# A four-layer graph network on one core: constant tiles for row numbers and list places, queries in two parts, layer 0's keys in another PSUM bank and its u8 conversions behind the copies

## The chip, the cores and the metric

The kernel runs on one core of a Trainium2 chip. The metric is the device time of one execution in microseconds (us); lower is better. The engines are named as in the profile: PE is TensorE (matmuls; PEld its weight loads), DVE is VectorE, ACT is ScalarE, POOL is GpSimd, SP is SyncE, which here only issues DMAs. Each engine takes its instructions from a queue of its own, and engines wait for one another by semaphores.

## What is computed

A node matrix x of 4096 x 256 and a symmetric 0/1 adjacency of 4096 x 4096 (about 0.8% ones) go through four graph layers, each followed by a residual add and a layer norm. All of it is fp32.

```python
# layer 0
deg = adj.sum(1, keepdims=True)
x = LN(x + relu(concat([x, adj @ x / max(deg, 1)]) @ W0 + b0))
# layer 1: two steps; R = (adj + I) / row sums, A = top-p attention
for n in range(2):
    q, k = Xa @ W1.T @ W2.T, Xa @ W3.T
    probs = softmax(q @ k.T)
    A = probs on the smallest set of largest entries whose mass reaches 0.9, renormalised
    Xf, Xa = R @ Xf, A @ Xa
    Z += Xf @ U1[n].T + Xa @ U2[n].T
x = LN(x + LN(x + Z))
# layer 2
x = LN(x + concat([x, adj @ x, diag(adj @ adj)]) @ W2 + b2)
# layer 3
x = LN(x + relu(D^-1/2 (adj + I) D^-1/2 @ x @ W3 + b3))
```

## The kernel before

Rows are worked in NT = 32 tiles of 128. A matrix that multiplies the adjacency is kept as an upper and a lower half in fp32r side by side, so one product with a 128 x 128 block of the adjacency is a matmul of 512 columns into one PSUM bank.

The code is traced tile by tile and a scheduler then fixes the order of each engine's queue: mainly the order of the text, with later instructions put forward where earlier ones are expected to wait. Buffers come from pools: a name (tag) with `bufs` buffers is used in turn, and an instruction that writes a buffer waits until the readers of its former content are done.

**Layer 0** (lines 207 to 297). `l0_main(it)` loads the tile's adjacency from POOL's queue in four pieces of 512 KB (L129; four buffers in all, so exactly one tile), and TensorE runs 32 matmuls over them (L160). `partial` does three things with each piece: ACT casts it to u8 (L234, two buffers) and SP stores that to DRAM for layer 1 (L235); DVE adds it into `sums` (L239, L241, L244). A piece's buffer is free when matmuls, cast and sums are done with it. `l0_degrees` makes the degree with a one-column matmul (L251), then its clipped reciprocal (`rd`), `rs` = 1/(deg + 1) and `dinv` = (deg + 1)^-0.5, the last on POOL (L259). `l0_agg` scales the product; `l0_end` loads x again (L270, on ACT's queue), transposes x and the product on TensorE (L170), copies the result from PSUM on ACT (`xt`, L172), multiplies with W0 (L274), and does bias, relu, residual and norm on DVE with the power on POOL (L184), and stores x1 and x1b by SP (L282, L283). `l0_keys` transposes the new rows, copies (L172), multiplies with W3 (L201), and splits the keys into an upper and a lower half (`upk` L194, L203 on ACT, L204 on DVE). L201 and L274 both write `mm_bank`, one PSUM bank used in two halves by turns. In iteration `it` of the loop the order of the text is: degrees and product of tile it-1, main of tile it, keys of tile it-2, end of tile it-1.

**Layer 1** (lines 300 to 994). `run_step` goes through the tiles with a pipeline of three: in iteration i, tile i+2 gets its logits (`logits_chunk`, L358: two matmuls for each of eight chunks g of 512 keys, then a copy to `e` on ACT, L359); tile i+1 is judged (row maximum from MAX8 of each group L377, exponentials L396/L400, the largest entries L472/L474, threshold, `flag`); tile i is multiplied (gathered rows in step 0, L616 and L703; transposed probabilities in step 1, L686 and L711). R times Xf runs beside it (L629, L632) and in step 0 the diagonal for layer 2 (L638, with the adjacency loaded again, L129). A dictionary `ops` hangs small pieces of work behind chunk g: `at(g, f)`. Among these: g = 1 is `mix` for the tile finished before (L764), g = 4 is `flag`, and g = 6 is `query` of tile i+3: transpose, copy (L172), matmul with the joined W1, W2 into `mm_bank` (L338), upper half on DVE (`upk`, L194), cast on ACT (L341) and lower half on DVE (L342). The q that comes out is what L358 of the next iteration multiplies.

`flag` (L526) decides which rows of a tile need another treatment and writes their row numbers into a list in DRAM (`list_d`) by an indirect DMA from POOL (L550): `at` holds each row's place in the list (L543) and `ids` its row number (L544), both tiles of 128 x 1 made anew for each tile, with four buffers. `ids` is computed from the constant `spare` and the tile's number alone. Rows on the list are worked through by `put_off` and `left_over` later.

**Layers 2 and 3** (lines 997 to 1061) run the adjacency product again, tile by tile; the change leaves them alone, but for `dinv` that they read.

Of the kernel before, what the change touches and what calls it, by code (L numbers as in the profile page):

```python
# [2 lines left out]

# [1 line left out]

# [6 lines left out]
F32 = mybir.dt.float32  # L12
I32 = mybir.dt.int32
# [8 lines left out]
P = 128  # L22
# [26 lines left out]
def gnn_stack(ctx, tc, x, adjt, adjn, w0, b0, w1, w2t, w3t, u1t, u2t, ln_g, ln_b, w2, b2, w3, b3, out):  # L49
# [114 lines left out]
    def transposed(*srcs):  # L164

        n = 2 * len(srcs)
        ps = ps_tr.tile([P, 4, P], F32, tag="tr", name="tr")
        for s, src in enumerate(srcs):
            for c in range(2):
                nc.tensor.transpose(ps[:, 2 * s + c, :], src[:, c * P : (c + 1) * P], ident)  # L170
        t = work.tile([P, 4, P], F32, tag="xt", name="xt")
        nc.scalar.copy(t[:, :n, :], ps[:, :n, :])  # L172
        return t

    def ln_stats(t):
# [20 lines left out]

    def make_keys(xt, dst):

        ps = half("mm")
        for c in range(2):  # L200
            nc.tensor.matmul(ps[:, :P], w3t_sb[:, c, :], xt[:, c, :], start=(c == 0), stop=(c == 1))  # L201
        up = upper(ps[:, :P])
        nc.scalar.copy(dst[:DA, :], up[:DA, :])  # L203
        nc.vector.tensor_sub(dst[DA:, :], ps[DA:, :P], up[DA:, :])  # L204


    with tc.tile_pool(name="l0", bufs=1) as l0, tc.tile_pool(name="l0w", bufs=2) as l0w:
        x0h = load_halves(l0.tile([P, 4 * J0 * D], F32, name="scratch"), x, nc.scalar)
        w0_sb = load_w(l0, w0, "w0_sb")
        lb_sb = load_bcast(l0, ln_b, "lb_sb")  # L210
        b0_sb = load_bcast(l0, b0, "b0_sb")

        w1_sb = l0.tile([DA, D], F32, name="w1_sb")
        nc.scalar.dma_start(w1_sb, w1)
        w2t_sb = l0.tile([DA, DA], F32, name="w2t_sb")
        nc.scalar.dma_start(w2t_sb, w2t)
        for c in range(2):
            ps = half("mm")
            nc.tensor.matmul(ps[:, :DA], w1_sb[:, c * P : (c + 1) * P], w2t_sb, start=True, stop=True)
            for h in range(2):  # L220
                nc.scalar.copy(wq_sb[:, c, h * DA : (h + 1) * DA], ps[:, :DA])
        for h in range(2):
            nc.scalar.dma_start(w3t_sb[:, :, h * DA : (h + 1) * DA], w3t.rearrange("(c p) o -> p c o", p=P))
        x1 = xpool.tile([P, NT, D], F32, tag="X", name="x1")

        def l0_main(it):
            acc = ps_acc.tile([P, 512], F32, tag=("acc", "nef")[it % 2], name="acc")

            W = J0 * P
            sums = l0w.tile([P, W], F32, tag="sums", name="sums")  # L230

            def partial(c, a):
                a8 = l0w.tile([P, JP, P], U8, tag="a8", name="a8")
                nc.scalar.copy(a8, a.bitcast(F32))  # L234
                nc.sync.dma_start(adj8_d[it][:, c * JP : (c + 1) * JP, :], a8)  # L235
                a = a.bitcast(F32).rearrange("p j i -> p (j i)")
                for k in range(0, JP * P, W):
                    if c == 0 and k == W:
                        nc.vector.tensor_add(sums, a[:, :W], a[:, W : 2 * W])  # L239
                    elif c > 0:  # L240
                        nc.vector.tensor_add(sums, sums, a[:, k : k + W])  # L241
                if c + 1 == NJP:
                    for k in (W // 2, W // 4):
                        nc.vector.tensor_add(sums[:, :k], sums[:, :k], sums[:, k : 2 * k])  # L244

            adj_matmul(l0w, acc, it, lambda jt: x0h[:, jt, :], JP, partial)
            return acc, sums

        def l0_degrees(it, sums):
            pd = half("acc")  # L250
            nc.tensor.matmul(pd[:, 0:1], sums[:, :P], ones_col, start=True, stop=True)  # L251
            deg = pd[:, 0:1]
            rd = work.tile([P, 1], F32, tag="rdeg", name="rdeg")
            nc.vector.tensor_scalar(rd, deg, 1.0, None, op0=ALU.max)
            nc.vector.reciprocal(rd, rd)
            d1 = work.tile([P, 1], F32, tag="deg1", name="deg1")
            nc.vector.tensor_scalar(d1, deg, 1.0, None, op0=ALU.add)
            nc.vector.reciprocal(rs[:, it : it + 1], d1)
            nc.gpsimd.tensor_tensor(dinv[:, it : it + 1], d1, mhalf, op=ALU.pow)  # L259
            return rd  # L260

        def l0_agg(acc, rd):
            agg = l0w.tile([P, D], F32, tag="agg", name="agg")
            nc.scalar.activation(agg, acc[:, :D], AF.Copy, scale=rd)
            nc.vector.scalar_tensor_tensor(agg, acc[:, D:], rd, agg, op0=ALU.mult, op1=ALU.add)
            return agg

        def l0_end(it, agg):
            xi = l0w.tile([P, D], F32, tag="x0i", name="x0i")
            nc.scalar.dma_start(xi, rows(x, it))  # L270
            xt = transposed(xi, agg)
            ps = half("mm")
            for c in range(4):
                nc.tensor.matmul(ps, xt[:, c, :], w0_sb[:, c, :], start=(c == 0), stop=(c == 3))  # L274
# [12 lines left out]

        acc = None
        for it in range(NT + 2):
            if 1 <= it <= NT:  # L290
                agg = l0_agg(acc, l0_degrees(it - 1, sums))
            if it < NT:
                acc, sums = l0_main(it)
            if it >= 2:
                l0_keys(it - 2)
            if 1 <= it <= NT:
                l0_end(it - 1, agg)


    with tc.tile_pool(name="l1", bufs=1, reuse_waits="tile") as l1:  # L300
# [20 lines left out]
        nc.vector.memset(spare0, 0.0)  # L321
        blank = l1.tile([P, NT], I32, name="blank")
        nc.gpsimd.iota(blank, pattern=[[0, NT]], base=N, channel_multiplier=1)
        for t in list_d:
            nc.sync.dma_start(t[:N, :].rearrange("(k p) o -> p (k o)", p=P), blank)

# [3 lines left out]
                nc.scalar.dma_start(t, src[n].rearrange("(c p) o -> p c o", p=P))  # L330
                cur[name] = t

        def query(xi):

            xt = transposed(xi)
            ps = half("mm")
            for c in range(2):
                nc.tensor.matmul(ps[:, :P], wq_sb[:, c, :], xt[:, c, :], start=(c == 0), stop=(c == 1))  # L338
            up = upper(ps[:, :P])
            q = [work.tile([P, P], F32R, tag=f"q{k}", name=f"q{k}", bufs=3) for k in range(2)]  # L340
            nc.scalar.copy(q[0], up)  # L341
            nc.vector.tensor_sub(q[1], ps[:, :P], up)  # L342
            return q
# [182 lines left out]
        def flag(st):  # L526
# [17 lines left out]
            nc.vector.tensor_scalar(ids, spare, float(st["tile"] * P - N), None, op0=ALU.add)  # L544
            later["base"] = sofar
            if st["tile"] == NT - 1:

                st["to"] = to = small("to_last", 1, I32, 1)
                nc.vector.scalar_tensor_tensor(to, st["bad"], float(P), ids, op0=ALU.mult, op1=ALU.add)
            nc.gpsimd.indirect_dma_start(  # L550
                out=list_d[cur["n"]], out_offset=bass.IndirectOffsetOnAxis(ap=at[:, 0:1], axis=0), in_=ids, in_offset=None)

        def bit_by_bit(st):

# [302 lines left out]
        def run_step(n, es):  # L857
# [31 lines left out]
            for i in range(-2, NT):  # L889
# [213 lines left out]
```

## Time and profile before

| | |
|---|---|
| timed runs | 3653.54, 3656.0, 3663.65 us (median 3656.0) |
| span of the profiled execution | 3611.7 us |
| busy DVE / ACT / POOL | 65% / 41% / 28% of the span |
| layer 0 | to about 484 us (last degree matmul) |
| step 0 of layer 1 | to about 1510 us |
| lists and turn to step 1 | to about 1770 us |
| step 1 of layer 1 | to about 2985 us |
| layers 2 and 3 | to the end |

The profile is of one execution. "Busy" is time in which an engine worked; a wait line names the engine and line that waited, what ended the wait, the total, how often and the longest. In a line in order of time the columns are start, duration, engine, line and operation, what was written and read, the count, and in brackets the idle time before and what ended it. The granted clock is the share of full speed that TensorE was given.

### The profile page before, as it was taken

The numbers are of one execution on the slowest core, as the hardware profiler recorded it, in microseconds if no ns is written. First come the engines' busy times: TensorE is split into PE (matmuls) and PEld (weight loads), VectorE is DVE, ScalarE is ACT, GpSimd is POOL, SyncE is SP. The second block draws the span as 40 slices with busy tenths as digits, with TensorE's granted clock in tenths as the row PEclk, the third lists the DMA queues.
The fourth block names the chain that finished last, engine by engine and source line by source line (L and its number), as shares of the span: only waits on it lengthen the run. The fifth ranks groups of instructions, "written<-read, shape, count | busy, mean of one in ns | idle before, by whom it ended". The sixth has DMA issues, their size and how long they took to land. (4 is left out here: it accounts for less than half of the span.)

```text
span 3611.7 us, 46113 instructions
## 1 busy us (share of the span) xinstructions
PE 3114.6 (86%) x14780; PEld 2528.6 (70%) x14780; DVE 2364.5 (65%) x7144; ACT 1464.9 (41%) x2590; POOL 1005.1 (28%) x1328
## 2 busy tenths in 40 slices
PE   7777857898899899868898989999999737999998
PEld 5666645777777777646777777777788625887776
DVE  5566545776767777734688889799889673434333
ACT  3343334554545555444544545555465301111000
POOL 1222203666666666610000000100101012222332
PEclk8999978999999999988999999999999868999999
DMA  7777665676667767723000012011111007887887
GB/s 225 207 217 210 203 93 155 156 178 171 170 163 179 176 176 177 177 86 116 28 23 23 26 31 40 24 31 34 34 33 33 17 19 231 246 246 241 269 271 227
DMA packets 269343, 484.19 MB, mean 134 GB/s; under 512 B 44096, under 2 KB 186240, under 8 KB 269088
## 3 DMA queue, kind: packets, MB, share of 16 engines
q0 software_dynamic: 101760, 339.45, 34.5%
q1 hardware_dynamic: 150352, 125.73, 12.7%
q10 hardware_dynamic: 16976, 15.95, 1.5%
q8 instruction: 120, 1.97, 0.2%
q14 instruction: 135, 1.11, 0.1%
HBM read 423.45 MB, written 57.54 MB: 133 GB/s over the span
## 5 line engine op out<-in xcount | busy, mean ns | idle before, releaser
L632 PE MATMUL acc_r<-xh,adjq 128*128 128x512 f32 x2048 | 639.3, 444 | 49.1 <-ACT adjq L629 36.8
L616 POOL DMA_INDIRECT G<-x_d,cols x512 | 496.3, 969 | 355.1 <-PE acc_bank L703 262.9
L711 PE MATMUL acc_bank<-xa,at 128*128 128x256 f32 x2304 | 569.5, 387 | 18.0 <-ACT at L689 17.5
L160 PE MATMUL acc<-xh,adjt 128*128 128x512 f32 x2048 | 544.3, 416 | 45.4 <-DVE xh L137 29.4
L632 PEld LDWEIGHTS acc_r<-xh,adjq 128*128 128x128 f32 x2048 | 395.2, 199 | 152.8 <-ACT adjq L629 61.4
L358 PE MATMUL lg<-kS,q 128*128 128x512 f32 x1104 | 407.8, 456 | 97.7 <-ACT q L341 83.7
L160 PEld LDWEIGHTS acc<-xh,adjt 128*128 128x128 f32 x2048 | 391.8, 196 | 136.2 <-ACT xh L136 31.2
L711 PEld LDWEIGHTS acc_bank<-xa,at 128*128 128x128 f32 x2304 | 424.5, 194 | 80.1 <-ACT at L689 28.9
L629 ACT CAST adjq<-adj 128x512 fp32r<-128x512 uint8 x512 | 315.3, 619 | 387.3 <-issue 128.4
L377 DVE MAX8 cand<-e 128x8 f32<-128x256 f32 x1024 | 384.0, 415 | 40.1 <-ACT e L359 39.0
L129 POOL DMA_DIRECT2D adjt<-in_adjt x384 | 208.6, 544 | 695.4 <-PE acc L160 392.9
L359 ACT COPY e<-lg 128x512 f32<-128x512 f32 x552 | 317.8, 584 | 166.9 <-PE lg L358 164.8
L184 POOL TENSOR_TENSOR rstd<-ve,mhalf 128x1 f32<-128x1 f32 x168 | 102.7, 611 | 800.4 <-DVE ve L182 747.9
L703 PE MATMUL acc_bank<-G,dg 128*128 128x256 f32 x1024 | 292.6, 403 | 16.3 <-DMA G<-x_d,cols 11.0
L474 DVE FIND_INDEX8 cols<-top,e 128x8 uint32<-128x4096 f32 x64 | 282.8, 4419 | 0.0
L358 PEld LDWEIGHTS lg<-kS,q 128*128 128x128 f32 x1104 | 190.7, 199 | 124.9 <-ACT q L341 90.2
L160 PE MATMUL acc<-yh,adjt 128*128 128x512 f32 x1024 | 256.0, 402 | 2.5 <-DMA adjt<-in_adjt 2.1
L234 ACT CAST a<-adjt 128x1024 uint8<-128x1024 f32 x128 | 133.9, 1046 | 271.8 <-DMA adjt<-in_adjt 128.3
L689 ACT COPY at<-at_ps 128x512 f32<-128x512 f32 x296 | 172.4, 589 | 175.9 <-PE at_ps L686 175.4
L703 PEld LDWEIGHTS acc_bank<-G,dg 128*128 128x128 f32 x1024 | 201.5, 200 | 58.1 <-DMA G<-x_d,cols 11.3
L160 PEld LDWEIGHTS acc<-yh,adjt 128*128 128x128 f32 x1024 | 190.0, 188 | 47.2 <-DMA adjt<-in_adjt 2.8
L686 PE MATMUL at_ps<-ident,e 128*128 128x128 f32 x1184 | 184.3, 279 | 40.9 <-DVE e L607 25.3
(270 smaller groups left out, 4515.5 us busy)
## 6 DMA issues: line engine op xcount, KB each, us to landing
adjt<-in_adjt POOLq DMA_DIRECT2D x384, 512.0 KB, 5.0
adjn<-in_adjn POOLq DMA_DIRECT2D x128, 512.0 KB, 5.6
adj<-adj_d SPq DMA_DIRECT2D x256, 128.0 KB, 3.0
adj_d<-a SPq DMA_DIRECT2D x128, 128.0 KB, 3.9
x_d<-x SPq DMA_DIRECT2D x64, 128.0 KB, 4.9
xf_d<-xf_new SPq DMA_DIRECT2D x64, 128.0 KB, 2.9
G<-x_d,cols POOLq DMA_INDIRECT x512, 4.4
xf<-xf_d SPq DMA_DIRECT2D x64, 128.0 KB, 2.0
```

The lines of the kernel that those rows point to most:

```text
L129: nc.gpsimd.dma_start(t, src[it, :, c * jp : (c + 1) * jp, :])
L160: nc.tensor.matmul(acc, a[:, j, :], halves(jt), start=(jt == 0), stop=(jt == NT - 1))
L358: nc.tensor.matmul(pl[:, :LC], q[k], kS[:, s], start=(k == 0), stop=(k == 1))
L359: nc.scalar.copy(l[:, s], pl[:, :LC])
L377: nc.vector.max(dst[:, 8 * g : 8 * g + 8], src[:, g * GW : (g + 1) * GW])
L474: nc.vector.max_index(st["at"][:, 8 * r : 8 * r + 8], t8, st["e"][:, :N])
L616: nc.gpsimd.indirect_dma_start(out=g, out_offset=None, in_=x1_d, in_offset=bass.IndirectOffsetOnAxis(ap=st["at"][:, k : k + 1], axis=0))
L629: nc.scalar.copy(a, cur["a8"][:, g % 2 * GP : (g % 2 + 1) * GP, :])
L632: nc.tensor.matmul(acc_r, a[:, j, :], xf[:, jt, :], start=(jt == 0), stop=False)
L686: nc.tensor.transpose(ps[:, j, :], e[:, (g * G + j) * P : (g * G + j + 1) * P], ident)
L703: nc.tensor.matmul(acc_a, dg[:, k % 4, :], st["G"][k], start=(k == 0), stop=(k == KEPT - 1))
L711: nc.tensor.matmul(acc_a, ats[g][:, j, :], cur["xa"][:, jt, :], start=(jt == 0), stop=(jt == NT - 1))
```

## The change

Three things are changed. **In layer 1** `ids` becomes a constant tile of 128 x 32 row numbers, made once by an iota, of which a tile uses one column, and the list places become one column each of a 128 x 32 tile for each step (`slots_of`), so that neither comes from a pool of four buffers. **The query** is split: its transposes and copy come one group ahead of its matmul, at groups 5 and 6 in step 0 and at groups 0 and 1 in step 1 (before: both at 6). **In layer 0** the keys' product goes to a buffer of the logits' pool (`ps_lg`) in place of `mm_bank`, keys come three tiles behind the main product in place of two, with the last two after the loop; the casts to u8 and their stores leave `partial` and come after `l0_end` in the text, in `l0_bytes`, and ACT may issue them only after the copy `xt` of that `l0_end`; and deg + 1 is kept in a tile of 128 x 32, of which `dinv` is made by one power after the loop.

```diff
@@ transposed
-        nc.scalar.copy(t[:, :n, :], ps[:, :n, :])
+        turns["xt"] = nc.scalar.copy(t[:, :n, :], ps[:, :n, :])
@@ make_keys
-        ps = half("mm")
+        ps = ps_lg.tile([P, 512], F32, tag="lg", name="k_ps")
@@ layer 0
+        deg1 = l0.tile([P, NT], F32, name="deg1")
...
+            pieces = []
+
             def partial(c, a):
-                a8 = l0w.tile([P, JP, P], U8, tag="a8", name="a8")
-                nc.scalar.copy(a8, a.bitcast(F32))
-                nc.sync.dma_start(adj8_d[it][:, c * JP : (c + 1) * JP, :], a8)
+                pieces.append(a)
...
-            return acc, sums
+            return acc, sums, pieces
+
+        def l0_bytes(it, pieces):
+
+            with tc.issue_after(turns["xt"].ins) if it > 0 else nullcontext():
+                for c, a in enumerate(pieces):
+                    a8 = l0w.tile([P, JP, P], U8, tag="a8", name="a8")
+                    nc.scalar.copy(a8, a.bitcast(F32))
+                    nc.sync.dma_start(adj8_d[it][:, c * JP : (c + 1) * JP, :], a8)
...
-            d1 = work.tile([P, 1], F32, tag="deg1", name="deg1")
+            d1 = deg1[:, it : it + 1]
...
-            nc.gpsimd.tensor_tensor(dinv[:, it : it + 1], d1, mhalf, op=ALU.pow)
...
-        for it in range(NT + 2):
-            if 1 <= it <= NT:
+        for it in range(NT + 1):
+            if it >= 1:
                 agg = l0_agg(acc, l0_degrees(it - 1, sums))
             if it < NT:
-                acc, sums = l0_main(it)
-            if it >= 2:
-                l0_keys(it - 2)
-            if 1 <= it <= NT:
+                acc, sums, adj_pieces = l0_main(it)
+            if it >= 3:
+                l0_keys(it - 3)
+            if it >= 1:
                 l0_end(it - 1, agg)
+            if it < NT:
+                l0_bytes(it, adj_pieces)
+        nc.gpsimd.tensor_tensor(dinv, deg1, mhalf.to_broadcast([P, NT]), op=ALU.pow)
+        l0_keys(NT - 2)
+        l0_keys(NT - 1)
@@ layer 1
+        ids = l1.tile([P, NT], I32, name="ids")
+        nc.gpsimd.iota(ids, pattern=[[P, NT]], base=0, channel_multiplier=1)
+        slots_of = [l1.tile([P, NT], I32, name=f"slots{n}") for n in range(STEPS)]
...
-        def query(xi):
-
-            xt = transposed(xi)
+        def query(xi, xt=None):
+
+            if xt is None:
+                xt = transposed(xi)
@@ flag
-            at, ids = small("at", 1, I32, 4), small("ids", 1, I32, 4)
+            i = st["tile"]
+            at, rows_i = slots_of[cur["n"]][:, i : i + 1], ids[:, i : i + 1]
...
-            nc.vector.tensor_scalar(ids, spare, float(st["tile"] * P - N), None, op0=ALU.add)
...
             nc.gpsimd.indirect_dma_start(
-                out=list_d[cur["n"]], out_offset=bass.IndirectOffsetOnAxis(ap=at[:, 0:1], axis=0), in_=ids, in_offset=None)
+                out=list_d[cur["n"]], out_offset=bass.IndirectOffsetOnAxis(ap=at, axis=0), in_=rows_i, in_offset=None)
@@ run_step
+                if 0 < i + 2 < NT - 1:
+                    turned = []
+                    g = 1 if n else 6
+                    at(g - 1, lambda i, turned: turned.append(transposed(cur["xa"][:, i + 3, :])), i, turned)
+                    at(g, lambda turned: cur["qs"].append(query(None, turned[0])), turned)
...
-                if 0 < i + 2 < NT - 1:
-                    at(6, lambda i: cur["qs"].append(query(cur["xa"][:, i + 3, :])), i)
```

More of the change, by code (lines that the diff above doesn't have):

```diff
@@ L1 @@
 import math
-from contextlib import ExitStack
+from contextlib import ExitStack, nullcontext
 import numpy as np
@@ L539, in flag @@
             nc.vector.tensor_add(sofar, later["base"], pb[:, 0:1])
-            at, ids = small("at", 1, I32, 4), small("ids", 1, I32, 4)
+            i = st["tile"]
+            at, rows_i = slots_of[cur["n"]][:, i : i + 1], ids[:, i : i + 1]
             nc.vector.scalar_tensor_tensor(slot, pb[:, 1:2], later["base"], spare, op0=ALU.add, op1=ALU.subtract)
             nc.vector.scalar_tensor_tensor(at, slot, st["bad"], spare, op0=ALU.mult, op1=ALU.add)
-            nc.vector.tensor_scalar(ids, spare, float(st["tile"] * P - N), None, op0=ALU.add)
             later["base"] = sofar
-            if st["tile"] == NT - 1:
+            if i == NT - 1:
                 st["to"] = to = small("to_last", 1, I32, 1)
-                nc.vector.scalar_tensor_tensor(to, st["bad"], float(P), ids, op0=ALU.mult, op1=ALU.add)
+                nc.vector.scalar_tensor_tensor(to, st["bad"], float(P), rows_i, op0=ALU.mult, op1=ALU.add)
             nc.gpsimd.indirect_dma_start(
-                out=list_d[cur["n"]], out_offset=bass.IndirectOffsetOnAxis(ap=at[:, 0:1], axis=0), in_=ids, in_offset=None)
+                out=list_d[cur["n"]], out_offset=bass.IndirectOffsetOnAxis(ap=at, axis=0), in_=rows_i, in_offset=None)
         def bit_by_bit(st):
```

## The prediction

> **What bounds the kernel now.** I read the page's busy line first, then busy time by stage, the waits of each stage, and one tile in order of time.
>
> ```profile
> PE 3114.6 (86%) x14780; PEld 2528.6 (70%) x14780; DVE 2364.5 (65%) x7144; ACT 1464.9 (41%) x2590; POOL 1005.1 (28%) x1328
> ```
>
> ```profile
> 58.00:470.00 412.00, 325.74 (x1463) 254.95 (x1461) 243.56 (x645) 155.43 (x226) 93.09 (x169) 0.95 0.70 207
> ...
> 742.80:1509.20 766.40, 692.65 (x3471) 577.14 (x3470) 540.47 (x1625) 390.47 (x774) 469.68 (x525) 0.95 0.70 174
> ...
> 1770.00:2000.00 230.00, 205.55 (x1045) 172.44 (x1044) 189.73 (x663) 113.24 (x189) 16.84 (x22) 0.97 0.08 23
> 2000.00:2885.00 885.00, 820.46 (x4099) 677.30 (x4099) 758.27 (x2488) 457.35 (x762) 75.61 (x87) 0.96 0.13 31
> ```
>
> The columns are the stretch, its length, then busy time of PE, its weight loads, DVE, ACT, POOL, then TensorE's granted clock, DMA share, GB/s. The rows are layer 0, the steady part of layer 1's step 0 (25 tiles), and step 1 in two parts. TensorE is never idle for long, so I look for what makes it wait. Waits in step 0 (total, times, longest):
>
> ```profile
> DVE ids L544 <- DMA list_d<-ids,at: 205.6, 28, 11.1
> ...
> ACT q L341 <- DVE upk L194: 83.9, 30, 5.5
> ...
> PE lg L358 <- ACT q L341: 61.5, 28, 4.8
> ```
>
> The three are one chain, seen in a tile in order of time:
>
> ```profile
> 1012.04 1.00 POOL L550 DMA_INDIRECT list_d<-ids,at  x1 [0.30 <-issue]
> ...
> 1016.08 0.71 PE L338 MATMUL mm_bank<-xt,wq_sb 128*128 128x128 f32 x4
> ...
> 1020.47 0.15 DVE L544 TENSOR_SCALAR ids<-spare 128x1 int32<-128x1 f32 x1 [8.31 <-DMA list_d<-ids,at]
> ...
> 1021.53 0.27 DVE L194 TENSOR_SCALAR upk<-mm_bank 128x128 int32<-128x128 int32 x1
> ...
> 1021.84 0.30 ACT L341 CAST q<-upk 128x128 fp32r<-128x128 f32 x1 [4.10 <-DVE upk L194]
> ```
>
> A later tile's `ids` is queued on DVE right behind this tile's work. Its buffer is still read by the scatter issued at 1012.04, which lands 8.4 us later. Behind it wait the last MAX8s and `upk`. The query matmul was done by 1016.8, but q comes at 1021.84, and the next tile's first logits start at 1022.19, after 3.42 us of idle TensorE. The clock then drops:
>
> ```profile
> 1022.20:1026.60 4.40, 4.40 (x10) 3.50 (x11) 4.40 (x11) 3.68 (x7) 1.76 (x2) 0.50 0.97 343
> ...
> 1035.90:1047.30 11.40, 11.40 (x64) 9.92 (x64) 6.70 (x33) 4.66 (x9) 8.02 (x9) 1.00 0.62 145
> ```
>
> Layer 0 has its own waits, about two per tile:
>
> ```profile
> ACT a L234 <- DMA adjt<-in_adjt: 128.3, 32, 6.1
> ...
> PE mm_bank L274 <- DVE kS L204: 44.0, 26, 2.8
> PE mm_bank L201 <- ACT xt L172: 41.2, 28, 4.9
> ```
>
> The copy `xt` (L172) stands on ACT behind a cast to u8 that waits for its piece (cast at 310.68, copies at 311.63, keys matmul at 312.05 after 1.43 us); L274 waits for the keys' readers, since both write one bank.
>
> **The Trainium skill.** "TensorE: Matmul & The Clock Gate", Part 1: the clock is at half or full rate and falls to half after an idle window of some 3.4 us. The trace agrees: 0.50 in the stretch above, in pieces of 3.4 us. "PSUM — Partial Sum Buffer", Engine vs sequencer instructions: ScalarE, VectorE and GpSimd queues are strict FIFO; so `upk` can't pass `ids`, as seen. The same page, PSUM bank collisions raise a hardware error: two engines may not touch one bank at once, so it is guarded by bank; hence L274's wait for readers of the other half. "DMA: Bandwidth & Descriptors", Anatomy of one DMA — SWDGE (gpsimd) path: about 2.0 us plus bytes/436e3. That gives 2.0 us for a 512-byte scatter and 3.2 for a 512 KB piece; the trace has 8.3 and 4.7, and these are used.
>
> **The change, part by part**, against the profiled span of 3611.7 us; the timed median of 3656.0 is 1.2% above it, so I scale by 1.0123 at the end.
>
> *ids and list places, step 0.* Removed: 64 writes of 0.153 us (9.8 us of DVE) and their wait. Added: one iota of 128x32, 0.16 us by `blank`'s row, on POOL before step 0, hidden by the loads there. `at` becomes a column, written 30 us after the previous scatter, which landed 8.3 us after its issue: no new wait. A tile takes 766.4/25 = 30.66 us. From one first-logits start to the next, typical groups of the tile are 4.37, 3.08, 5.76 (with the mix), then 2.71, 3.11, 2.73, 2.86, and 3.5 for the last without its wait. Warm, the first takes 2.7. But the first three cannot simply shrink by 1.67: in the tile at 1145.57, which waited little, they took 3.15, 3.08, 6.98, again 13.2 in all. There the mix (L764) waits for its `xt` copy, queued on ACT behind four exponentials, and these wait for the row maximum behind the same `ids`. Without the wait the maximum comes after the last copied chunk (1016.5), about 0.75 of MAX8s, 0.28 and 0.14: 1017.9 instead of 1023.2, so 5.3 earlier, while the next tile starts 3.5 earlier. So the three take 13.2 - 1.8 = 11.4 (TensorE's own floor: 2.7 + 3.1 + 5.25 = 11.05). New tile: 11.4 + 11.4 + 3.5 = 26.3; I take 26.4. Other engines fit: DVE 21.6 (82%), POOL 18.8, DMA share 0.70 x 30.66/26.4 = 0.81, as in layers 2 and 3. Gain 25 x 4.25 = 106; the 14.2 us of the same wait in two tiles between 560 and 722 give some 9 more: **115 us**. Bounds: 45 (tile at 29, rival 2) and 140.
>
> *Query in two parts.* In step 0 the transposes go one group ahead and the matmul stays; this removes at most the 0.28 us that L338 waits, already in the sum. In step 1 it goes from group 6 to groups 0 and 1. There nine waits for q cost 24.4 us and half clock in five of them 5 x 1.7 = 8.5: 33 us at most. Against it: DVE is 83 to 86% busy, TensorE waits 19.2 us for `bad` (L536), and the query now shares a bank with the mix in group 1, whose reader L766 stands behind a 4.4 us MATCH_REPLACE8. Bounds -20 to +33, value **20 us**. The `ids` waits of 26.8 us between 1510 and 1770 lie mostly beside gathers and loads: **5 us**.
>
> *Layer 0: pow.* Thirty-two of 0.567 us leave POOL, where the adjacency loads queue; before them it waits 58.8 us for DVE, yet the next load is then held by TensorE's use of its buffer, so this is worth nothing. One pow of 128x32 comes at the end, between 0.57 and 18 us, read only in layer 2: nothing.
>
> *Layer 0: keys in another bank.* Frees up to 44.0 us of L274's wait. Keys come one iteration later; their tail after the loop stays two tiles.
>
> *Layer 0: casts and stores.* Per tile four casts of 1.05 on ACT and four stores on SP move past the transposes' copies and, in the text, past the stores of x1 and x1b. This frees up to 41.2 us of L201's wait. But a cast also releases its piece's buffer, and the four buffers are one tile. If end(k-1) is transposed only after all of tile k's matmuls, the next loads start then: copies 1.8, casts 1.05 each, the third waiting for a u8 buffer (store 3.9 us): its cast ends at 7.9, the fourth at 9.0; landing 4.9 later, and matmuls of 1.85 each: 9.0 + 4.9 + 1.85 and tails = 16.6 us per tile. If it is transposed while TensorE waits for pieces, the loop is copy to cast 1.05, load 4.9, two pieces 3.7, transposes and copy 1.0 = 10.7. Now a tile takes (483.6 - 58.0)/29 = 14.7 although TensorE's own work is 10.9 (32 matmuls at 0.229, and 3.6 of transposes, degrees, keys and L274), so 3.8 of queue mismatch. The new order has the same floor with a longer loop through ACT, and I expect the two patterns to mix: (10.7 + 16.6)/2 = 13.7, plus part of the mismatch: no change. Value **0**, bounds +105 (to 11.3 a tile) and -60.
>
> Sum: 115 + 20 + 5 + 0 = 140; 3611.7 - 140 = 3472; times 1.0123 = **3515 us**.
>
> **Rivals.** (1) The forecast, 0.55, own range 3460 to 3580. (2) Another wait takes the place of `ids` in step 0 (ACT's exponentials, or POOL's gathers at 0.97 us each): tile at 29 us, gain 45, sum 60: 3595. For it: DVE's and ACT's queues are close-packed; against: DVE idles 152 us on `ids` in 21 tiles, far more than TensorE loses. 0.20. (3) Layer 0 comes near its floor as well, 105 more: 3410. For: its 85 us of named waits; against: loads now hang on late casts. 0.15. (4) Slower: SP sends the u8 stores behind x1 and x1b, in their order in the text; these wait for the norm some 7 us after the copies, so the third cast waits till about 11, and a tile takes 20 us: 31 x 5.3 = 164 lost, more than the 140 gained: about 3680. It decides from 19.2 us a tile. Against: the trace's SP order sends what is ready first. 0.08. (5) The column write waits for the scatter just as `ids` did: no change, about 3650, 0.02.
>
> **Numbers.** Faster by over 0.3% (about what this measurement can tell from no change) is 1 + 2 + 3 = 0.90, same 0.02, slower 0.08. The range takes rivals 1 and 2 and half of 3: 3415 to 3605.
>
> **What would show it.** Step 0 tiles of 26 to 27 us, no DVE wait on a list DMA, no wait of L358 for q, no half clock there; DVE above 80%. Step 1: q's wait gone, waits for the bank in group 1 at most as long. Layer 0: no cast ahead of `xt`; its end time against 484 us says which pattern won. Wrong if step 0 stays above 29 us a tile or layer 0 ends past 560.

## Result and profile after

The changed kernel takes 3618.9 us (median of 4 runs, 3612.1 to 3622.2), and the kernel before 3657.0 (3653.5 to 3663.7) on the same chip. The ratio is **0.9891, interval 0.987 to 0.991**: 38 us faster where 141 were forecast, and outside the range of 3415 to 3605. The profiled execution of the changed kernel spans 3619.1 us.

First the busy line of its page:

```profile
PE 3132.5 (87%) x14780; PEld 2541.3 (70%) x14780; DVE 2375.5 (66%) x7080; ACT 1473.0 (41%) x2590; POOL 993.5 (27%) x1298
```

The shares say nothing new; the 64 instructions that DVE has lost are the writes of `ids`. Then busy time by stage, in the columns used before: layer 0, 25 tiles of step 0, and step 1 in two parts.

```profile
58.00:462.00 404.00, 349.37 (x1533) 270.81 (x1532) 253.82 (x671) 160.75 (x232) 82.88 (x145) 0.95 0.72 219
...
734.40:1520.10 785.70, 698.60 (x3471) 585.89 (x3470) 550.08 (x1598) 397.18 (x774) 471.99 (x524) 0.93 0.70 170
...
1751.50:1973.10 221.60, 212.93 (x1126) 179.61 (x1124) 184.99 (x633) 113.76 (x192) 16.79 (x22) 1.00 0.08 23
1973.10:2804.80 831.70, 771.72 (x3847) 635.87 (x3845) 719.18 (x2391) 439.80 (x734) 66.90 (x81) 0.97 0.13 31
```

Layer 0 ends at 462.0 and not at 483.6. Step 0, where 106 us were to be gained, takes 785.7 us for 25 tiles, 31.4 each, against 30.66 before, and the granted clock there is 0.93 and not 0.95. Its waits, by engine and line waited for (total, times, longest):

```profile
PE nef_ps L656 <- DMA adjn<-in_adjn: 55.3, 21, 4.3
PEld nef_ps L656 <- issue: 46.8, 17, 4.7
...
PE acc_r L650 <- DVE xf_new L666: 14.6, 13, 2.3
```

No DVE wait for the list is left, and none of `lg` for `q`. In its place TensorE waits for the **adjacency piece of step 0's second product** (`adjn`, 512 KB), once in nearly every tile. One of these waits in order of time (POOL and TensorE):

```profile
1005.27 1.00 POOL L568 DMA_INDIRECT list_d<-ids,slots  x1 [0.30 <-issue]
...
1008.78 0.61 POOL L129 DMA_DIRECT2D adjn<-in_adjn  x1
...
1018.11 1.08 PE L656 MATMUL nef_ps<-adjn,adjq 128*128 128x128 f32 x4 [3.66 <-DMA adjn<-in_adjn]
```

The list scatter is issued at 1005.27, the next piece 3.5 us later, and the piece's first matmul starts 9.3 us after that. The 4.7 us that I had named for a piece is the median of layer 0's pieces in the trace of before; step 0's pieces in that same trace have a median of 5.6 us and take up to 10.5.

My theory after this: **the scatter holds the DMA queues up for some ten microseconds, so the piece behind it is late; before the change TensorE's wait for `ids` covered that lateness.** The rival: the pieces are late by themselves, through their two buffers and the gathers ahead of them on POOL.

### The profile page after: what moved, and what is told of

The parts are those of the page before. It is cut to its first block, busy times and chain, and to the rows that moved or that the text cites. A ratio compares the mean times of both kernels' runs of the same rounds, so it can differ in the third digit from the quotient of the medians.

```text
span 3619.1 us, 46089 instructions
## 1 busy us (share of the span) xinstructions
PE 3132.5 (87%) x14780; PEld 2541.3 (70%) x14780; DVE 2375.5 (66%) x7080; ACT 1473.0 (41%) x2590; POOL 993.5 (27%) x1298
## 5 line engine op out<-in xcount | busy, mean ns | idle before, releaser
L160 PEld LDWEIGHTS acc<-xh,adjt 128*128 128x128 f32 x2048 | 400.6, 200 | 204.3 <-DMA adjt<-in_adjt 73.4
L376 PE MATMUL lg<-kS,q 128*128 128x512 f32 x1104 | 403.4, 452 | 10.5 <-ACT q L359 5.7
L656 PEld LDWEIGHTS nef_ps<-adjn,adjq 128*128 128x128 f32 x1024 | 162.1, 206 | 116.5 <-issue 53.1
L656 PE MATMUL nef_ps<-adjn,adjq 128*128 128x128 f32 x1024 | 159.3, 281 | 84.8 <-DMA adjn<-in_adjn 73.2
```

The lines of the kernel that those rows point to most:

```text
L160: nc.tensor.matmul(acc, a[:, j, :], halves(jt), start=(jt == 0), stop=(jt == NT - 1))
L376: nc.tensor.matmul(pl[:, :LC], q[k], kS[:, s], start=(k == 0), stop=(k == 1))
L656: nc.tensor.matmul(pn[:, :P], a[:, j, :], cur["b"][:, jt % (2 * GP), :], start=(jt == 0), stop=(jt == NT - 1))
```

## Experiments

Each comparison ran on one chip beside the kernel before, whose median lay between 3606.6 and 3657.0 us in the six comparisons. So times are compared as ratios to it, and stages within a comparison.

### The three parts alone

The kernel before again, and with one of the change's three parts each; their diffs are the parts of the diff shown with the change (constant tiles; the query with its two `at` lines; all of layer 0's lines).

> The kernel before, profiled once more, because its first profile (span 3611.7 us) is 43 us shorter than its timed runs (3653 to 3664), while the profile of the changed kernel (3619.1) agrees with its timed runs. Every theory: time 3650 to 3665. If the first profile was one lucky execution, this one has a span near 3655 and the step-0 tiles of layer 1 are longer than 30.7 us (31.5 to 32); if profiling itself makes this kernel faster, the span is again near 3612.

> The kernel before with the constant row numbers and list places alone. Theory A (the list scatter holds up the software DMA queue for 8 to 10 us; the wait for ids only covered the late adjacency load behind it): the wait on the list DMA goes, a wait of the adjacency-matmul of step 0 (nef_ps) for its adjn load of 60 us or more comes, step-0 tile 30 to 31.5 us, time -25 to +10 us. Rival B (as predicted: the wait was the bound and its removal pays in full when alone; what the whole change lacks was eaten by its other parts): tile 26 to 28 us, time -90 to -120 us. Rival C (the late load comes of layer 0's or the query's part): no wait for adjn here above 25 us.

> The kernel before with the query in two parts alone. Theory A: step 1 (layer 1, from about 1510 us) shorter by 5 to 15 us, since its waits for q go but waits for at and bad remain; step 0 unchanged because the query there still stands behind ids: time -5 to -15 us. Rival B (my prediction's term): -20 us or more. Rival C (the query collides with the mix in its bank): 0 to +20 us.

> The kernel before with the layer 0 part alone (keys' bank, casts and stores behind the copies, one pow at the end). Theory A (layer 0 gains what the changed kernel's trace shows and nothing is lost elsewhere): layer 0's last degree matmul at 460 to 464 us against 483.6, time -18 to -25 us. Rival B (most of the whole change's -38 us is layer 0, and ids plus query nearly cancel): -30 to -40 us. Prediction: 0 within -105 and +60.

The repeat took 3628.2 us with a span of 3626.4, beside a median of 3631.7. A profile's span and the timed runs of the same chip agree here, so nothing is to be scaled; why the first profile's 3611.7 was shorter stays open. Ratios: ids alone **0.9878 (0.985 to 0.991)**, layer 0 alone **0.9932 (0.990 to 0.996)**, query alone **1.0133 (1.010 to 1.016)**, that is -46, -23 and +49 us; for the query the worst of the three expectations was +20. Stage lengths in us, from the starts of the last matmul of each tile of the second product (`ident_r`), and layer 0 from its last degree matmul:

| stage | before again | ids | query | layer 0 |
|---|---|---|---|---|
| layer 0 | 484.5 | 480.9 | 482.7 | 463.2 |
| to the steady part of step 0 | 261.2 | 256.7 | 262.1 | 269.6 |
| step 0, 25 tiles | 776.0 | 778.7 | 794.2 | 782.2 |
| to the steady part of step 1 | 237.5 | 231.8 | 237.3 | 234.5 |
| step 1 without second product | 252.7 | 226.1 | 260.0 | 249.8 |
| step 1 with second product | 808.2 | 805.3 | 834.6 | 814.5 |
| the rest | 806.3 | 801.7 | 810.3 | 812.2 |

So the constant row numbers gain **nothing in step 0**, where I had put 106 us, and 27 us early in step 1, where I had put none for them. (The profiled execution of layer0_alone is at the upper end of its runs, 3598 to 3628: layer 0's 21 us are there, and other stages, which the edit doesn't touch, are longer. The time is better known than the single profile.) TensorE's longest waits of step 0 in before again, and then in ids alone:

```profile
PE lg L358 <- ACT q L341: 65.8, 25, 4.3
```

```profile
PE nef_ps L642 <- DMA adjn<-in_adjn: 65.9, 19, 5.6
PEld nef_ps L642 <- issue: 53.7, 14, 6.0
```

One wait has taken the place of the other, with the same total. The new one comes with the `ids` edit alone, so neither of the other parts brings it. The waits early in step 1, before again and then with ids alone:

```profile
DVE ids L544 <- DMA list_d<-ids,at: 33.9, 8, 8.3
...
PE lg L358 <- ACT q L341: 25.3, 8, 5.3
```

```profile
PE lg L362 <- ACT q L345: 5.3, 1, 5.3
```

The waits for q that I had given to the query's split were made by `ids`; constant row numbers remove seven of eight.

### What the scatter does to other transfers

The trace has DMA-completion records, nearly complete in ids_alone. They give the time from issue to landing, by how long before it the last scatter was issued (step 0, medians; my sorting):

| us since the scatter's issue | adjacency piece, 512 KB | gather, 128 KB |
|---|---|---|
| 2.5 to 5 | 9.9 (23) | 9.4 (49) |
| 8 to 11 | 7.6 (24) | 6.9 (46) |
| 15 to 20 | 5.1 (18) | 2.8 (54) |

Transfers issued in the scatter's wake land some 5 to 7 us late. Sorted in the same way, before again has 9.9 us for its 23 pieces issued 2.5 to 5 us after a scatter: the lateness was there before the change, and TensorE, which stood waiting for q, waited only 4.0 us for `adjn` in all. Three edits on the changed kernel with the query back in one part (**ids_l0**) test it; that base first.

```diff
-                if 0 < i + 2 < NT - 1:
-                    turned = []
-                    g = 1 if n else 6
-                    at(g - 1, lambda i, turned: turned.append(transposed(cur["xa"][:, i + 3, :])), i, turned)
-                    at(g, lambda turned: cur["qs"].append(query(None, turned[0])), turned)
...
+                if 0 < i + 2 < NT - 1:
+                    at(6, lambda i: cur["qs"].append(query(cur["xa"][:, i + 3, :])), i)
```

> The changed kernel with the query back in one part at its old place (constant row numbers and layer 0's part stay). Theory A (the parts are separate stages and add up; the query in two parts costs time wherever it stands): 0.9878 x 0.9932 = 0.981 of before, about 3563 on the chip of the single parts, so some 30 us below the changed kernel. Rival B (the query's part is bad only while ids is waited for, and pays once that wait is gone): not below the changed kernel's 0.989.

Measured: **0.9806 (0.978 to 0.983)**, as the product of the two single ratios, 0.981. Next the scatter left out in step 0 (no_scatter), issued later (scatter_at_6), or writing rows of 64 bytes (scatter_64B).

```diff
             later["base"] = sofar
+            if cur["n"] == 0:
+                return
```

> ids_l0 without the list scatter in step 0 (its flagged rows then get no second pass in step 0; everything else is done). Theory A (the scatter holds all DMA engines for about 10 us, and the adjacency piece issued 3.5 us after it lands after 9.9 us in place of 4.8): no wait of nef_ps for adjn, step-0 tile 31 to 26.5-28 us, time 75 to 115 us below ids_l0. Rival B (the pieces are late because two buffers of 512 KB and the gathers' order on POOL make them late, whatever the scatter does): less than 20 us below ids_l0, tile 30 us or more.

The time is 1.0132 of before, 112 us above ids_l0, but not by step 0. With rows lacking their second pass, the other data send one later second pass of step 1 into the bit-by-bit search, where TensorE idles 182 us once. The largest group of DVE in that stretch:

```profile
L581 DVE SCALAR_TENSOR_TENSOR spare_row<-e,t_thr_l 128x4096 uint8<-128x4096 f32 x30 | 134.5, 4485 | 1.1
```

So only step 0 is read. Its row:

```profile
712.50:1422.00 709.50, 659.94 (x3471) 552.36 (x3470) 544.87 (x1598) 386.96 (x773) 442.15 (x499) 1.00 0.63 187
```

28.4 us a tile against 30.6 in ids_l0, the granted clock full (0.97 there), and next to no wait for `adjn` (47.5 us there). The rival falls: the buffers and the gathers were left as they are. But even without the scatter this is 2 us above my 26.4.

```diff
+            st["scatter"] = lambda: nc.gpsimd.indirect_dma_start(
...
                     at(4, flag, cd)
                     if n == 0:
+                        at(6, lambda cd: cd["scatter"](), cd)
```

> ids_l0 with step 0's scatter issued two groups later, just behind the last adjacency piece of its tile and ahead of the gathers of group 6, so that the next piece is issued 7 to 8 us after it and no longer 3.5. Theory A: a piece issued 8 to 11 us after a scatter landed in 7.6 us, which the matmuls two groups later can bear; tile 27 to 29 us, time 50 to 100 us below ids_l0. Rival B (order on POOL and the buffers): no change within 15 us. Rival C (the scatter now holds up the gathers and the first piece of the next tile): the wait only moves to acc_bank or to the next tile's piece, tile above 30 us.

0.9816 (0.980 to 0.984), 3571.6 us against ids_l0's 3571.9. The edit changed nothing: the place in the text doesn't decide POOL's order here, and that was the one of ids_l0, the scatter between the same two pieces. So this run tests no theory; it shows how well a time repeats. A later place was not tried again.

```diff
+            wide = rows_i
+            if cur["n"] == 0:
+                wide = cur["w"].tile([P, 16], I32, tag="wide", name="wide", bufs=2)
+                nc.vector.tensor_copy(wide, rows_i.to_broadcast([P, 16]))
...
-                out=list_d[cur["n"]], out_offset=bass.IndirectOffsetOnAxis(ap=at, axis=0), in_=rows_i, in_offset=None)
+                out=list_d[cur["n"]], out_offset=bass.IndirectOffsetOnAxis(ap=at, axis=0), in_=wide, in_offset=None)
```

> ids_l0 with step 0's list in rows of 64 bytes: the scatter writes 128 pieces of 64 bytes in place of 128 of 4 bytes, at its old place. Theory A1 (writes of 4 bytes to DRAM are what is slow[...]): the scatter lands in 3 to 5 us and not 8.4, the piece behind it in 5 to 6 us, tile 27 to 29 us. Theory A2 (what is slow is 128 single descriptors with scattered addresses, or the queue's own start, whatever their size): scatter 8 to 9 us, no change within 15 us.

**0.9672 (0.965 to 0.970)**: 50 us below ids_l0, tile 29.2 us. Pieces issued 2.5 to 5 us after the scatter land after about 4.4 us, as far as this trace's incomplete records tell; bank_ids_64B below, with the same rows and nearly complete records, has 4.6 (23 pieces). That could be by the size of a write, or because neighbouring entries no longer share a piece of memory: rows without a flag go to one spare place each, 128 four-byte entries in a row. Two more runs on ids_l0 tell these apart: entries 64 bytes apart of which only 4 bytes are written (its index is multiplied by 16, one more small DVE instruction per tile), and rows of 32 bytes from a constant tile.

```diff
+                at16 = cur["w"].tile([P, 1], I32, tag="at16", name="at16", bufs=4)
+                nc.vector.tensor_scalar(at16, at, 16.0, None, op0=ALU.mult)
+                at = at16
```

> ids_l0 with each list entry in a 64-byte row of its own, but only its first 4 bytes written. Theory A1 (a write of 4 bytes is slow by its size): the scatter lands after 8 to 9 us, tile 30 to 31 us, ratio 0.978 to 0.985 as ids_l0. Theory A3 (what is slow is that 16 neighbouring entries lie in the same 64 bytes and are written from several queues): scatter about 3 us, tile 29 to 29.5 us, ratio 0.965 to 0.970 as scatter_64B.

```diff
+                    cur["wide"] = cur["w"].tile([P, NT, 8], I32, tag="wide", name="wide", bufs=1)
+                    nc.gpsimd.iota(cur["wide"], pattern=[[P, NT], [0, 8]], base=0, channel_multiplier=1)
...
+            wide = rows_i if cur["n"] else cur["wide"][:, i, :]
```

> ids_l0 with step 0's list in rows of 32 bytes, all 32 written, from a constant tile. If what is slow is that several entries share 64 bytes: two rows still share, the scatter lands between 3 and 8 us, tile 29.5 to 31 us, ratio 0.972 to 0.981. If the shared unit is 32 bytes or less, or sixteen sharers are what it takes: scatter about 3 us, tile 29 to 29.5 us, ratio 0.965 to 0.970.

Four bytes, 64 apart: **0.9682 (0.966 to 0.971)**, as the 64-byte rows, so the size of the write is not it; what matters is how far the entries lie apart. Why neighbours are slow no run shows. Rows of 32 bytes: **0.9541 (0.951 to 0.957)** on another chip, of which more below; 32 bytes apart is enough, and less was not tried. What the queues show (issues between 750 and 1370 us, with median us to landing), first ids_alone, then scatter_32B:

```profile
adjn<-in_adjn POOLq DMA_DIRECT2D x79, 512.0 KB, 7.4
adj<-adj_d SPq DMA_DIRECT2D x79, 128.0 KB, 5.6
...
list_d<-ids,slots POOLq DMA_INDIRECT x20, 9.1
```

```profile
adjn<-in_adjn POOLq DMA_DIRECT2D x90, 512.0 KB, 5.0
adj<-adj_d SPq DMA_DIRECT2D x91, 128.0 KB, 3.5
...
list_d<-wide,slots POOLq DMA_INDIRECT x23, 2.6
```

The scatter lands in 2.6 us and not 9.1 although it writes eight times as much, and SP's loads, which are in another queue, are faster too: it was not the software queue alone that was held, as I had thought at first, but SP's as well. The two kernels ran on different chips, but ids_alone shows the same within one trace: SP's loads issued up to 2.5 us after a scatter take 7.9 us, and those issued 20 us or more after it 3.2. The Trainium skill's fixed cost of a DMA on this path, some 2.0 us ("DMA: Bandwidth & Descriptors", Anatomy of one DMA — SWDGE (gpsimd) path), is near the 2.6 and far from the 9.1.

### The query in two parts

The changed kernel, split query included, with the edit of scatter_64B:

> The changed kernel, query in two parts included, with step 0's list in rows of 64 bytes. The split query cost about 20 us in step 0 and 27 us in step 1 (profiles of the changed kernel against ids_l0). Theory C (in step 0 it does so by putting TensorE's waiting together in one piece of over 2 us per tile, each of which is followed by 3.4 us at half clock: 21 such pieces against 10): with the late adjacency pieces gone there is nothing to put together, step-0 tile 29 to 29.6 us as in scatter_64B (29.2), and only step 1's 20 to 30 us remain: ratio 0.973 to 0.977. Rival D (the split costs 0.8 us a tile in step 0 by its own work or order): tile 30 us, ratio 0.980 or more. Rival E (with the loads on time the split pays as predicted): ratio 0.966 or less.

**0.9726 (0.970 to 0.975)**, beside 0.9682 for scatter_4B_apart on the same chip, which differs from it by the query (and by 4 or 64 bytes): 14 us between the medians, 3524.0 and 3510.2. Step 0's tile is 29.0 us, 29.4 in scatter_4B_apart: with the loads on time the split costs nothing there, while step 1's stretch with the second product takes 825.4 us against 804.7. The 18 us that query_alone lost in step 0 appear where `ids` is still waited for; how was not tested further.

What it costs in the changed kernel itself, on one chip:

> The changed kernel once more, beside the two below on one chip: ratio 0.986 to 0.992, step-0 tile 31 to 31.6 us if the first result holds on this chip too.

> The changed kernel with the query in one part (ids_l0 again). If the split costs what the single parts and the stages say: 30 to 48 us, 0.8 to 1.3%, below changed_again on this chip. If the difference between 0.9891 and 0.9806 was the chip's: within 0.3% of changed_again.

0.9872 (0.986 to 0.989) and **0.9792 (0.978 to 0.981)**: the split costs 30 us in the whole change. Step 1 with second product, with the split and without:

```profile
1932.20:2756.80 824.60, 768.51 (x3846) 633.26 (x3844) 719.11 (x2391) 439.62 (x734) 68.08 (x81) 0.98 0.13 31
```

```profile
1938.70:2740.20 801.50, 762.01 (x3847) 630.82 (x3846) 713.70 (x2372) 434.22 (x732) 69.68 (x80) 0.99 0.14 32
```

23 of the profiles' 24 us lie here; step 0 is the same (756.7 and 756.5), and the stretch without second product gains 3.7. The waits of these two stretches, in the same order:

```profile
ACT e L418 <- DVE m L428: 16.2, 4, 6.3
DVE from_l L821 <- DMA to_l<-list_d: 15.7, 3, 6.0
...
PE mm_bank L782 <- ACT xt L172: 6.0, 1, 6.0
```

```profile
DVE from_l L820 <- DMA to_l<-list_d: 4.6, 1, 4.6
ACT e L417 <- DVE m L427: 4.2, 5, 1.6
...
PE mm_bank L781 <- ACT xt L172: 0.5, 1, 0.5
```

One of them in order of time:

```profile
2238.26 0.15 DVE L821 TENSOR_SCALAR from_l<-to_l 128x1 int32<-128x1 int32 x1 [5.15 <-DMA to_l<-list_d]
...
2241.28 3.71 ACT L418 ACTIVATE e<-e,m 128x4096 f32<-128x4096 f32 x1 [6.30 <-DVE m L428]
...
2244.99 0.56 ACT L172 COPY xt<-tr 128x512 f32<-128x512 f32 x1
...
2245.60 1.65 PE L782 MATMUL mm_bank<-u,xt 128*128 128x256 f32 x3 [6.04 <-ACT xt L172]
```

With the split, DVE more often reaches a second pass's first instruction before its list has landed (three times, not once); the row maximum stands behind it, ACT's exponential waits for the maximum, and the mix's copy `xt`, or a copy of transposed probabilities, waits behind the exponential. Of the 23 us, TensorE's idle time is 16.6 (56.1 against 39.5) and longer busy time 6.5; two waits behind such a list read, the one shown and one of 6.3 us at 1938.9, make 12.3 of the idle time. But the kernel before, with its query in one part, has such waits too (10.5 us of the mix for `xt` in before again), and its stretch is 808.2 us. So the chain is one that the split brings about more often than these kernels without it do, and not the split's alone. Whether that comes of the move to groups 0 and 1 or of the split, on after_64B:

```diff
-                    g = 1 if n else 6
+                    g = 6
```

> after_64B (the changed kernel with rows of 64 bytes) with step 1's query in two parts at groups 5 and 6 in place of 0 and 1. Theory F (the move to groups 0 and 1 is what costs: there the query's copies join ACT's queue at the exponential and the mix of the same tile): step 1's stretch with the second product back from 825 to 805-812 us, ratio 0.966 to 0.969. Rival G (the split itself costs, by the transposes' copy held longer): ratio 0.972 to 0.975.

0.9578 (0.955 to 0.961), beside 0.9541 for scatter_32B on that chip, which has no split (and rows of 32 bytes): 14 us, and the stretch takes 817.0 against 802.0, above the 805 to 812 of Theory F. So the move is the smaller part at most: 15 us of this stretch's 21 to 23 stay at groups 5 and 6, and in time nothing was won, again with two waits of the mix for `xt` (12.7 us). That the reordering behind the list's reads is the cause is read from the waits; no run took it away.

### Layer 0's two edits

The keys' bank alone, and the casts with their stores alone, each on the kernel before:

```diff
-        ps = half("mm")
+        ps = ps_lg.tile([P, 512], F32, tag="lg", name="k_ps")
```

> The kernel before with layer 0's keys in the other bank alone (same iteration, same order of casts). If the 44 us that L274 waited for the keys' readers were the gain of layer 0: last degree matmul 20 to 25 us below 483.6, and the casts alone give nothing. If the wait only moves (to the xt copy behind the cast): 0 to 5 us.

```diff
-                a8 = l0w.tile([P, JP, P], U8, tag="a8", name="a8")
-                nc.scalar.copy(a8, a.bitcast(F32))
-                nc.sync.dma_start(adj8_d[it][:, c * JP : (c + 1) * JP, :], a8)
+                pieces.append(a)
...
                 l0_end(it - 1, agg)
+            if it < NT:
+                l0_bytes(it, adj_pieces)
```

> The kernel before with layer 0's casts to u8 and their stores behind the copies alone. My prediction: two patterns of 16.6 and 10.7 us that mix to 13.7 a tile, no gain. If the casts ahead of xt were what cost layer 0 its time: last degree matmul 15 to 25 us below 483.6 and tiles that alternate between about 17 and 10 us as in the changed kernel. If it takes both edits: 0 to 8 us here and in keys_bank_alone.

The bank alone: **0.992 (0.989 to 0.995)**, layer 0 ends at 454.1. The casts alone: **1.0234 (1.020 to 1.027)**, layer 0 ends at 569.3, and after the first two every tile takes 17.0 to 18.5 us, which none of its three expectations foresaw: the slow one of the two patterns, with no mixing. With both, it ends at 463.2 and tiles alternate between about 17.3 and 9.8. TensorE's main waits between 26 and 450 us for the bank, the casts, and both (layer0_alone):

```profile
PE k_ps L201 <- ACT xt L172: 35.5, 24, 5.7
PE tr L170 <- DVE x L189: 31.9, 29, 2.3
```

```profile
PE acc L160 <- DMA adjt<-in_adjt: 97.9, 27, 4.4
```

```profile
PE acc L160 <- DMA adjt<-in_adjt: 44.5, 30, 2.8
```

The late casts hold the pieces' buffers, as I had worked out, and the next loads are late. Beside the bank they replace the waits for `xt` and for the norm's `x` by waits for loads, and gain little or nothing by it: on the chip of scatter_32B layer 0 ends at 454.2 with bank and casts and at 458.9 with the bank alone (bank_ids_64B, below), and on the chip of changed_again at 457.2 and 459.4; on a third, five kernels with both end it at 454.8 to 457.4 and one at 452.0, and the bank alone at 454.1. The two single ratios, 0.992 and 0.9932, agree within their intervals. Layer 0's gain is the bank's.

### What the runs point to

Row numbers as constants, the keys' bank, and list rows of 64 bytes; no casts behind the copies, no pow at the end, no split query.

> The kernel before with three edits: constant row numbers and list places, layer 0's keys in the other bank (casts, pow and query as before), and step 0's list in rows of 64 bytes. Theory (the parts add): layer 0's last degree matmul at 454 us, step-0 tile 29.2 us, ratio 0.963 to 0.968. Rival (the casts behind the copies help once the keys have their bank): layer 0 as in casts plus bank (456) or later, ratio 0.968 to 0.972.

> bank_ids_64B again. If the 27.3 us tile is the kernel's: ratio 0.950 to 0.956, tile 27.3. If it was the chip's: tile 28.5 to 29.5 and ratio 0.962 to 0.968 on a chip where the others behave as on the first ones.

**0.9526 (0.950 to 0.956)** on one chip, **0.9702 (0.969 to 0.972)** on another, there beside the changed kernel at 0.9872. On both it beats the kernel before by more than the interval, and on the second, where the changed kernel ran too, that one as well. The list of step 1 was left with neighbouring entries of 4 bytes in all these runs. Step 0 on the first chip, 24 tiles:

```profile
717.70:1373.10 655.40, 625.06 (x3331) 528.62 (x3330) 525.56 (x1557) 371.15 (x742) 453.78 (x504) 1.00 0.67 195
```

27.3 us a tile, nearly every tile alike, and the one wait left on TensorE is the mix's for `xt` (31.4 us, 25 times). On the other chip the same kernel takes 29.3, with tiles from 27.6 to 32.2, and its ratio is a little above the 0.962 to 0.968 expected there. The three kernels of the first chip's comparison all have 27.3 or less, so it goes with that chip or with something else that this comparison shares, not with the kernel; the instructions that I compared take the same time on both, and what differs was not found.

## Why the prediction was wrong

**Constant row numbers in step 0: 115 us forecast, about 2 measured** (776.0 to 778.7 in the steady part, 4.5 gained ahead of it). The step that failed is "Other engines fit: ... DMA share 0.70 x 30.66/26.4 = 0.81". A mean share says nothing of one load: I took a piece as 4.7 us wherever it stood, while each tile has one that is issued 3.5 us behind the scatter and lands after 9.9. Its lateness was in the kernel before too (9.9 us in before again), under the wait for q: 65.8 us of that wait went and 65.9 us of wait for `adjn` came. The trace at hand had said so, with step 0's pieces at up to 10.5 us. The mechanism of Rival 2 came true, a wait in the place of `ids`, but I had named ACT's exponentials or POOL's gathers for it, and its 29 us tile was still too short; its sum of 60 is also 10 less than its own terms, 45 + 20 + 5.

**The tile of 26.4 us.** With the wait really gone, the tile is 28.4 to 29.4 us in three comparisons and 27.3 in one, where TensorE is busy 26.0 of it (625.1/24). There the rest, 1.3 us, is the mix's wait for `xt`, which I had let go with the row maximum's wait. Beside scatter_4B_apart and after_64B, in one comparison on one chip, ran two kernels with step 0 as before (keys_bank_alone 30.7, casts_alone 30.6): against them, 29.4 and 29.0 are 1.2 to 1.7 us of the 4.25 forecast. On the chip of the 27.3 no step 0 of before was profiled. The change got none of it because it left the scatter as it was.

**Row numbers after step 0: 5 us forecast, 32 measured.** The 5 were for the turn to step 1, and 5.7 came there; the other 26.6 came early in step 1, where I had put none for them. I gave the waits for q between 1770 and 2000 to the query's place. They were the same chain as in step 0, `upk` behind `ids` on DVE, which I had just described; the cause was written down and then not carried to the next stage.

**Query in two parts: 20 us gain forecast, bounds -20 to +33; 49 lost alone and 30 lost in the whole.** The 33 us that it could gain belonged to the line above. What I had weighed against it, DVE's load and the shared bank, is not where it lost: the waits are in ACT's queue, behind an exponential. That the loss in the whole change lies in step 1's stretch with the second product is shown (23 of 24 us; of query_alone's longer profile about half), its chain only argued.

**Layer 0: 0 forecast, 21 us gained in the profile, 23 in the time.** The two patterns came as worked out: 16.6 forecast and 17.3 measured, 10.7 and about 9.8, mixed as forecast in the change, and 17 in every tile with the casts alone. Two terms were mis-sized. The clause "plus part of the mismatch: no change" filled my own 13.7 us a tile up to the 14.7 of before; 13.7 is what the changed kernel takes. And I let the bank's "up to 44.0 us" count for nothing; alone it gave 28 us of time (0.992) and 13.6 us a tile. The pow at the end had no run of its own.

**The scale of 1.0123** had no ground: it took one short execution for a property of the profile, and the kernel before has medians from 3606.6 to 3657.0 us on the chips of these comparisons.

**The signs.** Faster was right at 0.90, but by luck: -46 and -23 with the query's +30 make -39, near the -38 measured, and none of the three came from where it was forecast. The sign set for being wrong, step 0 above 29 us a tile, came with 31.4. Rival 4 did not come: SP issues a u8 store 0.03 us after its cast in the median and 2.1 us at most. Rivals 3 and 5 did not either; DVE waits for no list in step 0. One reading of the clock was too simple: in step 0 of the kernel before, 19 stretches at half clock begin during or right after idle pieces of TensorE of 1.6 to 3.9 us, and 17 of these are under 3.4 us. So it is the slow stretch that comes in pieces of 3.4 us here (16 of one piece, 3 of two); less idleness than that was enough to bring it on.

## What to carry over

Before a wait is removed, ask what else lands while it lasts: list each transfer's landing by its place in the tile, and not by one median. An indirect DMA that writes small entries next to each other can slow the loads of other queues for some ten microseconds; here 32 bytes for each entry were enough. And parts of a change that gain and lose cancel unseen: run each alone before the sum is explained.

## What the runs showed of the hardware

- A scatter of 128 neighbouring entries of 4 bytes lands after 8 to 9 us, and loads issued in that time land late, in SP's queue too (7.9 us for 128 KB, against 3.2 later). With full rows of 32 or 64 bytes (scatter_32B, bank_ids_64B) it lands after 2.6 us, and 512 KB loads behind it take 4.6 us. With 4 bytes written at a distance of 64 bytes the time and the tile are those of the full rows; that trace's few landings of the scatter lie between 2.0 and 3.7 us.
- In step 0 of the kernel before, TensorE's clock fell to half around idle pieces as short as 1.6 us.
- One and the same kernel ran at 0.953 of the kernel before on one chip and 0.970 on another, both with narrow intervals: a ratio of two kernels measured on one chip need not hold on another. Whether the chip itself is the cause was not found.
